# Layer 0's queries: x sent in by feature, with means and deviations sent through memory, in place of turning the normalised x on TensorE

## The chip, the cores and the metric

The kernel runs on one core of one Trainium2 chip. The time is device microseconds (us) of one execution, from its start to its end. Engines are named as the profile names them: PE (TensorE's matmuls), PEld (its weight loads), DVE (VectorE), ACT (ScalarE), POOL (GpSimd) and SP (SyncE, which issues most DMAs).

## The reference

Two layers of cross-attention and feed-forward over x of 2 x 2048 x 512, all float32. What matters here is layer 0's attention: its queries come from a doubly normalised x, its keys and values from a short context of 2 x 128 rows.

```python
def layer_norm(x, g, b):
    m = jnp.mean(x, axis=-1, keepdims=True)
    v = jnp.var(x, axis=-1, keepdims=True)
    return (x - m) * jax.lax.rsqrt(v + EPS) * g + b
...
q = layer_norm(query_sequences, ln_g, ln_b)      # query_sequences = _layernorm(x)
qh = (q @ Wq).reshape(N, t, N_HEADS, D_HEAD).transpose(0, 2, 1, 3)
qh = rope(qh); kh = rope(kh)
aw = jnp.einsum('nhtd,nhTd->nhtT', qh, kh) * (1.0 / jnp.sqrt(jnp.float32(D_HEAD)))
aw = GROK_SCALE * jnp.tanh(aw / GROK_SCALE)      # then the masks
out = jnp.einsum('nhtT,nhTd->nhtd', jax.nn.softmax(aw, axis=-1), vh)
return out @ Wo
...
x = x + _L0_xattn_ref(_layernorm(x, axis=-1), ctx_1024, ctx_1024, ...)
x = x + _L0_ffn_ref(_layernorm(x, axis=-1), ...)      # fake-quantised: needs the largest |x| of all tokens
x = x + _L1_xattn_ref(_layernorm(x, axis=-1), ctx_1024, ctx_1024, ...)
x = x + _L1_ffn_ref(_layernorm(x, axis=-1), ...)      # one of 8 experts for each token
```

## The kernel before

x stays in SBUF for the whole run as 32 tiles of 128 tokens x 512 features (`xs`), a token to a partition. A matmul sums over partitions, so the query product needs x the other way, a feature to a partition.

Layer 0's attention goes over 16 blocks of 256 tokens (two tiles; `blocks`, L312) and, in each block, over 4 groups of 4 heads. A block and a group make one *unit* u (block k = u // 4, group g = u % 4); there are 64. The loop at L479 is software-pipelined. In one pass it does scores(u), both query products of unit u + 2 (`queries`, L352: even features, then odd ones), mixed(u - 1), which weighs the values, and projected(u - 2), the output product, in that order on PE.

- `normed(k)` (L319) takes a block's mean and variance on DVE and the reciprocal deviation on POOL, `centered(k)` (L330) writes the normalised tile xn on DVE, and `turned(k, c0)` (L338) turns two of the four feature chunks: four 128x128 transposes on PE into PSUM (L345), from which ACT writes xnT with the layer norm's scale and bias (L347). For block k + 1, turned stands at the end of units g = 0 and g = 1 of block k; normed and centered stand in g = 2, one block earlier.
- The query product's two halves are multiplied by the rope tables on DVE (L367 to L373, tiles rt, one buffer each) and put together on POOL (L372, L374, tile q).
- In `mixed`, DVE takes the reciprocal (L410) and writes att (L411); scores and mixed share the PSUM tile sc.
- PSUM's pool psm has two buffers for one tag, "m", which the query products pq and the transposes pt share in turn.
- In g = 1 `finished` (L425) adds the attention to x and takes the next statistics, and `largest` (L433) takes each token's largest value for the FFN's quantisation.
- The FFN's weights are quantised beside this, one piece in the units g = 3 and g = 0 (`quantised`, L267; loads w_in with two buffers and w_down with one), and turned by DMA in the following unit (L290, L303).

Inside L456's block the order on PE, DVE and ACT is that of the program. The order on POOL and SP is the scheduler's: it takes what is ready by its own reckoning, so an instruction can go out long before its place in the program.

Before the loop, blocks 0 and 1 are prepared between the key and value products (L457 to L478); 23 of the x tiles hold weights until then and are loaded last (L474). After the loop, the FFN section loads the context again on ACT's queue (L611), turns it on PE (L623) and copies it to ctxT (L624) for layer 1's keys, two of which stand ahead of `act_step` (L648): that takes the maximum over all tokens, with one transpose (L590), which the FFN's first quantised tiles wait for.

Of the kernel before, what the change touches and what calls it, by code (L numbers as in the profile page):

```python
# [11 lines left out]
F32 = mybir.dt.float32  # L12
# [5 lines left out]
AF = mybir.ActivationFunctionType  # L18
ALU = mybir.AluOpType
# [4 lines left out]
P = 128  # L24
B, S, T, D = 2, 2048, 128, 512
# [37 lines left out]
def two_layers(ctx: ExitStack, tc: tile.TileContext, a, out):  # L63
# [9 lines left out]
    def load(dst, src):  # L73
        nc.sync.dma_start(out=dst, in_=src)
# [27 lines left out]
    def center(dst, x, mean, scale):  # L102
        nc.vector.tensor_scalar(dst, x, mean, scale, ALU.subtract, ALU.mult)
# [7 lines left out]
    def transposed(psum, src, n=ND):  # L111

        pt = psum.tile([P, n, P], F32, name="pt", tag="m")
        for c in range(n):
            nc.tensor.transpose(pt[:, c, :], src[:, c * P : (c + 1) * P], ident)
        return pt
# [33 lines left out]
    with ExitStack() as l0:  # L150
# [40 lines left out]
                wk[g].append(w.rearrange("p (c o f) -> p c o f", c=2, o=2))  # L191
        for n in order[:NB0]:
            load(xs[n], x_in[n])
        for c in range(ND):
            wv.append([])
            for f in range(E0 // D):
                w = xs[homes[8 + 2 * c + f]]
                load(w, a["L0_xattn_Wv"][c * P : (c + 1) * P, f * D : (f + 1) * D])
                wv[c].append(w)
# [79 lines left out]


        def gate_up_in(name, i):
            w = wtmp.tile([P, D], F32, name="w_in", tag="w_in")
            load(w, a[name][i * P : (i + 1) * P, :])
            return w

# [26 lines left out]
        blocks = [(j, b) for j in range(S // B0) for b in range(B)]  # L312
        tiles = [[b * TPB + j * NB0 + t for t in range(NB0)] for j, b in blocks]
        nu = len(blocks) * NG
        norms, xns, xnTs, ropes, qs, prs, atts, pws = {}, {}, {}, {}, {}, {}, {}, {}

        sc = pss.tile([P, 4, 512], F32, name="sc")

        def normed(k):  # L319


            for t, n in enumerate(tiles[k]):
                mv = variance(xs[n])
                ve = small.tile([P, 1], F32, name="ve")
                nc.vector.tensor_scalar(ve, mv[:, 1:2], 1.0 + EPS, EPS * EPS, ALU.mult, ALU.add)
                rr = small.tile([P, 1], F32, name="rr")
                nc.gpsimd.tensor_tensor(rr, ve, minus_half, ALU.pow)
                norms[k, t] = mv, rr

        def centered(k):  # L330
            xns[k] = []
            for t, n in enumerate(tiles[k]):
                mv, rr = norms[k, t]
                xn = mid.tile([P, D], F32, name="xn")
                center(xn, xs[n], mv[:, 0:1], rr)
                xns[k].append(xn)

        def turned(k, c0):  # L338

            if c0 == 0:  # L340
                xnTs[k] = mid.tile([P, ND, B0], F32, name="xnT")
            pt = psm.tile([P, 2, B0], F32, name="pt", tag="m")
            for c in range(2):
                for t, xn in enumerate(xns[k]):
                    nc.tensor.transpose(pt[:, c, t * P : (t + 1) * P], xn[:, (c0 + c) * P : (c0 + c + 1) * P], ident)  # L345
            for c in range(2):
                nc.scalar.activation(  # L347
                    xnTs[k][:, c0 + c, :], pt[:, c, :], AF.Identity,
                    bias=lnb[:, c0 + c : c0 + c + 1], scale=lng[:, c0 + c : c0 + c + 1],
                )  # L350

        def queries(u, par):  # L352
# [23 lines left out]
        def scores(u):  # L376

            k, g = divmod(u, NG)
            j, b = blocks[k]
            for par, k_ in ((0, kTe), (1, kTo)):  # L380
                for h in range(4):
                    rows = slice(32 * h, 32 * h + 32)
                    nc.tensor.matmul(  # L383
                        sc[:, h, :B0], k_[rows, g, b * T : (b + 1) * T], qs[u][par][rows, :],
                        start=(par == 0), stop=(par == 1), tile_position=(32 * h, 0),
                    )
            prs[u] = pr = mid.tile([P, 4, B0], F32, name="pr")
            nc.scalar.activation(pr, sc[:, :, :B0], AF.Tanh, scale=1.0 / (math.sqrt(DH0) * GROK))  # L388

            nc.scalar.activation(pr, pr, AF.Exp, bias=pad[:, b : b + 1], scale=GROK)  # L390
            if j == 0:
                nc.gpsimd.affine_select(
                    out=pr[:, :, :P], in_=pr[:, :, :P], pattern=[[0, 4], [1, P]],
                    compare_op=ALU.is_ge, fill=0.0, base=0, channel_multiplier=-1,
                )
# [60 lines left out]
        with tc.manual_schedule(engines={E.PE, E.DVE, E.Activation}):  # L456
            context()  # L457
            for g in range(NG):
                keys(g)
                if g == 1:  # L460
                    normed(0)
                if g == 2:
                    centered(0)
            nc.vector.tensor_scalar(pad, padu, -1e30, None, ALU.mult)
            for c in range(0, ND, 2):
                turned(0, c)
            values(0, 0)
            values(0, 1)
            queries(0, 0)
            values(1, 0)  # L470
            normed(1)
            queries(0, 1)
            values(1, 1)
            for n in homes:  # L474
                load(xs[n], x_in[n])
            queries(1, 0)
            centered(1)
            queries(1, 1)  # L478
            for u in range(nu + 2):  # L479
                k, g = divmod(u, NG)  # L480
                if u < nu:
                    scores(u)
                if u + 2 < nu:
                    queries(u + 2, 0)
                elif 1 < u < nu:
                    projected(u - 2, 0)
                if 0 < u <= nu:
                    mixed(u - 1)
                if u + 2 < nu:
                    queries(u + 2, 1)  # L490
                if u > 1:
                    for t in range(0 if u + 2 < nu or u >= nu else 1, NB0):
                        projected(u - 2, t)
                if g < 2 and k + 1 < nblk:
                    turned(k + 1, 2 * g)
                if u in turns:
                    turns[u]()
                if u in diags:
                    diags[u]()
                if g == 1 and k > 0:  # L500
                    for t in range(NB0):
                        finished(k - 1, t)
                    largest(k - 1, 0)
                if g == 2:
                    if k > 0:
                        largest(k - 1, 1)
                    if k + 2 < nblk:
                        normed(k + 2)
                        centered(k + 2)
                if g in (0, NG - 1) and u > 1:  # L510
                    if makes and not loaded:
                        load_, args, _, _ = makes[0]
                        loaded.append(load_(*args))
                    elif makes:
                        _, _, make, args = makes.pop(0)
                        turns[u + 1] = make(loaded.pop(), *args)
                        if makes:
                            load_, args, _, _ = makes[0]
                            loaded.append(load_(*args))
                if nu - 5 <= u < nu - 1:  # L520
                    diags[u + 1] = steps_along(u - nu + 5)
                if u == NG:
                    for name, clip in clips.items():
                        kept[name] = const.tile([P, 1], F32, name=f"kept_{name}")
                        nc.scalar.activation(kept[name], clip, AF.Exp, scale=-1.0)
                        nc.vector.tensor_scalar(kept[name], kept[name], 1.0, None, ALU.add)
                        nc.vector.reciprocal(kept[name], kept[name])
                if u == nu - 2:
                    load(wk1, a["L1_xattn_WkT"].rearrange("(c p) f -> p c f", p=P))
                    load(wv1, a["L1_xattn_WvT"].rearrange("(c p) f -> p c f", p=P))  # L530
            largest(nblk - 1, 1)
# [67 lines left out]
    with ExitStack() as up:  # L599
# [3 lines left out]
        kv = up.enter_context(tc.tile_pool(name="kv1", bufs=1, reuse_waits="tile"))  # L603

        ctxT = kv.tile([P, ND, B * T], F32, name="ctxT")
        cxs = [kv.tile([P, D], F32, name=f"cx{b}") for b in range(B)]
        bk = kv.tile([P, ND], F32, name="bk")
        bvb = kv.tile([P, D], F32, name="bvb")

        for b in range(B):  # L610
            nc.scalar.dma_start(out=cxs[b], in_=a["ctx_1024"][b])  # L611
        nc.scalar.dma_start(out=bk, in_=a["L1_xattn_bk"].rearrange("(c p) -> p c", p=P))
        load(bvb, a["L1_xattn_bv"].partition_broadcast(P))
        load(wq1, a["L1_xattn_WqT"].rearrange("(c p) f -> p c f", p=P))
# [4 lines left out]
        load(masks, a["mask_scores"].rearrange("(j p) k -> p j k", p=P))  # L619


        for b in range(B):
            pt = transposed(psm, cxs[b])  # L623
            nc.scalar.copy(ctxT[:, :, b * T : (b + 1) * T], pt)  # L624
        def keys(f):
            pk = psm.tile([P, B * T], F32, name="pk", tag="m")
            for c in range(ND):
# [656 lines left out]
```

## Time and profile before

| what | value |
|---|---|
| median of 3 runs | 1642.7 us (1641.58 to 1642.99) |
| profiled execution, its own time | 1642.48 us |
| its span | 1640.8 us |
| granted TensorE clock, mean | 0.998 |
| L345, the block transposes on PE | 128, a median of 273 ns each as recorded, from 27.5 to 623.1 us |
| L347, ACT's pass out of PSUM | 64, a mean of 559 ns, 32.6 us in all |
| L103, DVE's centering of xn | 32, 542 ns in the middle, 949 at most |
| layer 0's attention, last output matmul | starts 678.84 us, 7.13 us long (16 matmuls) |
| HBM read, written | 78.96 MB, 41.76 MB |

Matmuls are pipelined: a recorded duration is longer than the share of PE's time that the matmul takes, so the cost of a group of matmuls is read from the distance between what stands before and behind it. "Idle before" in the profile is the engine's idle time ahead of an instruction, with what ended it. DVE's and ACT's rows are durations of single instructions.

### The profile page before, as it was taken

What the parts mean: (1) busy time and instruction counts of PE and PEld (TensorE: products, weight loads), DVE (VectorE), ACT (ScalarE), POOL (GpSimd) and SP (SyncE); (2) the same over time, 40 slices, a digit from 0 to 9 for tenths busy, and PEclk for the clock granted to TensorE, in tenths of its full rate; (3) what the DMA queues carried; (4) which work ended last, traced back from release to release, by engine and by line L of the source; (5) the groups of instructions that cost most, each with busy time, mean ns of one, the idle gap of its engine ahead of it and who ended that gap; (6) DMA issues with size and microseconds to landing.
All of it is one profiled execution on the core that took longest, in us unless ns stands there. A gap on an engine that the chain in (4) does not pass through costs nothing. (4 is left out here: it accounts for less than half of the span.)

```text
span 1640.8 us, 26515 instructions
## 1 busy us (share of the span) xinstructions
PE 1597.7 (97%) x9962; PEld 952.5 (58%) x9962; DVE 1185.9 (72%) x2290; ACT 686.3 (42%) x1539; POOL 437.5 (27%) x498
## 2 busy tenths in 40 slices
PE   7999999999999999989999999999999999999997
PEld 5666666665666666534443566666666666654543
DVE  3466666777777765689986678898999889876332
ACT  1222222222222222234436576666666665662332
POOL 2322222222222221110005632333333221224553
PEclk9999999999999999999999999999999999999999
DMA  9400111010100220556658650001000000113332
GB/s 318 151 17 22 28 26 27 20 27 20 27 20 14 54 37 1 161 161 183 186 175 294 235 204 16 27 20 33 21 27 20 21 14 21 40 47 103 125 124 67
DMA packets 123883, 128.61 MB, mean 78 GB/s; under 512 B 43857, under 2 KB 91433, under 8 KB 123756
## 3 DMA queue, kind: packets, MB, share of 16 engines
q1 hardware_dynamic: 114508, 107.03, 21.2%
q0 software_dynamic: 6240, 18.70, 3.6%
q8 instruction: 80, 1.31, 0.3%
q10 hardware_dynamic: 3008, 1.19, 0.3%
q14 instruction: 47, 0.39, 0.1%
HBM read 78.96 MB, written 41.76 MB: 74 GB/s over the span
## 5 line engine op out<-in xcount | busy, mean ns | idle before, releaser
L362 PE MATMUL pq<-xnT,wq 128*128 128x256 f32 x1024 | 254.4, 392 | 0.0
L420 PE MATMUL pw<-wo,att 128*128 128x512 f32 x512 | 230.9, 593 | 0.0
L362 PEld LDWEIGHTS pq<-xnT,wq 128*128 128x128 f32 x1024 | 184.6, 190 | 66.9 <-issue 46.7
L855 ACT ACTIVATE s<-s,mx 128x128 f32<-128x128 f32 x512 | 176.7, 387 | 18.1 <-DVE mx L846 18.1
L388 ACT ACTIVATE pr<-sc 128x1024 f32<-128x1024 f32 x64 | 65.5, 1024 | 237.8 <-PE sc L383 234.7
L372 POOL TENSOR_TENSOR q<-rt,rt 128x256 f32<-128x256 f32 x64 | 46.5, 726 | 410.5 <-DVE rt L371 410.5
L420 PEld LDWEIGHTS pw<-wo,att 128*128 128x128 f32 x512 | 97.0, 190 | 96.2 <-issue 89.8
L410 DVE RECIPROCAL rd<-sc 128x256 f32<-128x256 f32 x64 | 112.5, 1757 | 51.1 <-PE sc L404 51.1
L1119 PE MATMUL pz<-we,x 128*128 x312 | 140.7, 594 | 0.6 <-issue 0.5
L813 PE MATMUL pq<-xT,wq 128*128 128x256 f32 x512 | 124.1, 385 | 0.0
L347 ACT ACTIVATE xnT<-pt,lnb,lng 128x256 f32<-128x256 f32 x64 | 32.6, 559 | 216.1 <-PE pt L345 216.1
L367 DVE TENSOR_TENSOR rt<-pq,rope_cos 128x256 f32<-128x256 f32 x64 | 27.2, 425 | 130.8 <-PE pq L362 120.2
L905 PE MATMUL pw<-wo,oT 128*128 128x512 f32 x256 | 115.5, 594 | 1.6 <-DVE oT L897 1.6
L928 PE MATMUL pl<-wgate,xnT 128*128 128x512 f32 x256 | 115.1, 592 | 0.0
L813 PEld LDWEIGHTS pq<-xT,wq 128*128 128x128 f32 x512 | 94.9, 190 | 28.0 <-issue 13.6
L716 ACT ACTIVATE gate<-pg,gsc 128x512 f32<-128x512 f32 x88 | 60.5, 687 | 96.5 <-PE pg L711 85.8
L711 PE MATMUL pu<-xqT,wuT 128*128 128x512 bf16 x352 | 90.3, 379 | 5.3 <-DVE h L719 5.3
L91 DVE BATCH_NORM_STATS2 st<-x 128x6 f32<-128x512 f32 x130 | 89.6, 689 | 5.6 <-DMA x<-in_ctx 3.4
L841 DVE SCALAR_TENSOR_TENSOR s<-sc,keep 128x1024 f32<-128x1024 f32 x64 | 77.9, 1217 | 20.6 <-PE sc L833 20.6
L1123 DVE TENSOR_TENSOR x<-x,x 128x512 f32<-128x512 f32 x39 | 27.0, 692 | 90.0 <-ACT x L1122 89.8
L711 PE MATMUL pg<-xqT,wgT 128*128 128x512 bf16 x352 | 90.3, 379 | 0.0
L1119 PEld LDWEIGHTS pz<-we,x 128*128 128x128 f32 x312 | 56.4, 190 | 58.2 <-issue 57.9
(218 smaller groups left out, 2847.7 us busy)
## 6 DMA issues: line engine op xcount, KB each, us to landing
h_dram<-h SPq DMA_DIRECT2D x88, 256.0 KB
hq<-h_dram SPq DMA_DIRECT2D x31, 704.0 KB
x_dram<-x SPq DMA_DIRECT2D x32, 258.0 KB
x<-in_x SPq DMA_DIRECT2D x32, 256.0 KB
we<-in_L_ffn_We SPq DMA_DIRECT2D x8, 1024.0 KB
w_in<-in_L_ffn_w_gate SPq DMA_DIRECT2D x11, 256.0 KB
w_down<-in_L_ffn_w_down SPq DMA_DIRECT2D x4, 704.0 KB
w_in<-in_L_ffn_w_up SPq DMA_DIRECT2D x11, 256.0 KB
```

What stands on the lines that cost most here:

```text
L91: nc.vector.bn_stats(out=st, in_=x)
L362: nc.tensor.matmul(pq, wqs[c // 2][:, c % 2, par, g * P : (g + 1) * P], xnTs[k][:, c, :], start=(c == 0), stop=(c == ND - 1))
L388: nc.scalar.activation(pr, sc[:, :, :B0], AF.Tanh, scale=1.0 / (math.sqrt(DH0) * GROK))
L410: nc.vector.reciprocal(rd, sc[:, 0, B0:])
L420: nc.tensor.matmul(pw, atts[u][:, f, t * P : (t + 1) * P], wo[:, 2 * g + f, :], start=(g == 0 and f == 0), stop=(g == NG - 1 and f == 1),)
L711: nc.tensor.matmul(dst, w[:, c, i * P : (i + 1) * P], xqTs[blk][:, c, :], start=(c == 0), stop=(c == ND - 1),)
L813: nc.tensor.matmul(pq, wq1[:, c, f * P : (f + 1) * P], xTs[blk][:, c, :], start=(c == 0), stop=(c == ND - 1))
L841: nc.vector.scalar_tensor_tensor(s, sc[:, 2 * half : 2 * half + 2].rearrange("p r c k -> p (r c) k"), -MASKED, keeps[n].unsqueeze(1).to_br ...
L855: nc.scalar.activation(s[:, h, :], s[:, h, :], AF.Exp, bias=mx[:, h : h + 1], **accum)
L905: nc.tensor.matmul(pw, os_[n][:, c, :], wo1[:, c, :], start=(c == 0), stop=(c == ND - 1))
L928: nc.tensor.matmul(pl, xn2T[n][:, c, :], wgate[:, c, :], start=(c == 0), stop=(c == ND - 1))
L1119: nc.tensor.matmul(pz, ring[j][:, c, :], we[:, bass.ds(e, 1), c, :], start=(c == 0), stop=(c == ND - 1))
```

## The change

x is sent in a second time by the host, already by feature (`x_turned`: for each block of 256 tokens, 128 features on partitions x 4 chunks x 256 tokens). For blocks 2 to 15 a block of it is loaded with one DMA of 512 KB straight into xnT (three buffers now). The mean and the reciprocal deviation are a value per token, which now lies along the free dimension: the block's 512 values are written to memory and read back spread over all partitions (tile along, one buffer). POOL subtracts the mean, DVE multiplies by the deviation, and ACT applies scale and bias in place. normed(k + 2), the load, the write and the read now stand at the end of g = 0 of block k; centered(k + 1) and scaled(k + 1) stand in g = 0 of block k, four units behind normed(k + 1), and affine(k + 1) in g = 1. Blocks 0 and 1 are still turned by PE (`first_blocks`), block 1's whole in unit 1. w_in has one buffer. In the FFN section the context too comes in by feature, as one DMA straight into ctxT, and its eight transposes and two copies go.

```diff
@@ -191,6 +191,13 @@
                 wk[g].append(w.rearrange("p (c o f) -> p c o f", c=2, o=2))
...
+        xnTs = {}
+
+        def features_in(k):
+
+            xnTs[k] = mid.tile([P, ND, B0], F32, name="xnT", bufs=3)
+            load(xnTs[k], a["x_turned"][k // B, k % B])
+
...
@@ -279,7 +286,7 @@
 
 
         def gate_up_in(name, i):
-            w = wtmp.tile([P, D], F32, name="w_in", tag="w_in")
+            w = wtmp.tile([P, D], F32, name="w_in", tag="w_in", bufs=1)
...
@@ -312,41 +319,64 @@
         blocks = [(j, b) for j in range(S // B0) for b in range(B)]
         tiles = [[b * TPB + j * NB0 + t for t in range(NB0)] for j, b in blocks]
         nu = len(blocks) * NG
-        norms, xns, xnTs, ropes, qs, prs, atts, pws = {}, {}, {}, {}, {}, {}, {}, {}
+        stats, along, ropes, qs, prs, atts, pws = {}, {}, {}, {}, {}, {}, {}
+        stat_dram = dram.tile([len(blocks), NB0, 2, P], F32, name="stat_dram")
 
...
         def normed(k):
 
 
+            stats[k] = small.tile([P, NB0, 2], F32, name="stat")
             for t, n in enumerate(tiles[k]):
                 mv = variance(xs[n])
                 ve = small.tile([P, 1], F32, name="ve")
                 nc.vector.tensor_scalar(ve, mv[:, 1:2], 1.0 + EPS, EPS * EPS, ALU.mult, ALU.add)
-                rr = small.tile([P, 1], F32, name="rr")
-                nc.gpsimd.tensor_tensor(rr, ve, minus_half, ALU.pow)
-                norms[k, t] = mv, rr
+                nc.vector.tensor_copy(stats[k][:, t, 0:1], mv[:, 0:1])
+                nc.gpsimd.tensor_tensor(stats[k][:, t, 1:2], ve, minus_half, ALU.pow)
+            if k > 1:
+                features_in(k)
+                turned_in(k)
+
+        def turned_in(k):
+
+            nc.sync.dma_start(out=stat_dram[k].rearrange("t s p -> p (t s)"), in_=stats[k].rearrange("p t s -> p (t s)"))
+            along[k] = mid.tile([P, NB0, 2, P], F32, name="along", bufs=1)
+            load(along[k], stat_dram[k].partition_broadcast(P))
+
+        def by_token(k, i, op, engine):
+            x = xnTs[k].rearrange("p c (t q) -> p c t q", t=NB0)
+            engine.tensor_tensor(x, x, along[k][:, :, i].unsqueeze(1).to_broadcast([P, ND, NB0, P]), op)
 
         def centered(k):
-            xns[k] = []
+            by_token(k, 0, ALU.subtract, nc.gpsimd)
+
+        def scaled(k):
+            by_token(k, 1, ALU.mult, nc.vector)
+
+        def first_blocks(k):
+
+            xn = mid.tile([P, NB0, D], F32, name="xn", tag="xnT", bufs=3)
             for t, n in enumerate(tiles[k]):
-                mv, rr = norms[k, t]
-                xn = mid.tile([P, D], F32, name="xn")
-                center(xn, xs[n], mv[:, 0:1], rr)
-                xns[k].append(xn)
-
-        def turned(k, c0):
-
-            if c0 == 0:
-                xnTs[k] = mid.tile([P, ND, B0], F32, name="xnT")
-            pt = psm.tile([P, 2, B0], F32, name="pt", tag="m")
-            for c in range(2):
-                for t, xn in enumerate(xns[k]):
-                    nc.tensor.transpose(pt[:, c, t * P : (t + 1) * P], xn[:, (c0 + c) * P : (c0 + c + 1) * P], ident)
-            for c in range(2):
+                center(xn[:, t, :], xs[n], stats[k][:, t, 0:1], stats[k][:, t, 1:2])
+            xnTs[k] = mid.tile([P, ND, B0], F32, name="xnT", bufs=3)
+
+            def rest():
+                for c0 in range(0, ND, 2):
+                    pt = psm.tile([P, 2, B0], F32, name="pt", tag="m")
+                    for c in range(2):
+                        for t in range(NB0):
+                            nc.tensor.transpose(
+                                pt[:, c, t * P : (t + 1) * P], xn[:, t, (c0 + c) * P : (c0 + c + 1) * P], ident
+                            )
+                    affine(k, c0, pt)
+
+            return rest
+
+        def affine(k, c0, pt=None):
+            for c in range(c0, c0 + 2):
                 nc.scalar.activation(
-                    xnTs[k][:, c0 + c, :], pt[:, c, :], AF.Identity,
-                    bias=lnb[:, c0 + c : c0 + c + 1], scale=lng[:, c0 + c : c0 + c + 1],
+                    xnTs[k][:, c, :], xnTs[k][:, c, :] if pt is None else pt[:, c - c0, :], AF.Identity, bias=lnb[:, c : c + 1], scale=lng[:, c : c + 1]
                 )
 
...
@@ -460,10 +490,9 @@
                 if g == 1:
                     normed(0)
                 if g == 2:
-                    centered(0)
+                    turn = first_blocks(0)
...
-            for c in range(0, ND, 2):
-                turned(0, c)
+            turn()
...
@@ -474,12 +503,13 @@
             for n in homes:
                 load(xs[n], x_in[n])
             queries(1, 0)
-            centered(1)
             queries(1, 1)
             for u in range(nu + 2):
                 k, g = divmod(u, NG)
                 if u < nu:
                     scores(u)
+                if g == 0 and 0 < k < nblk - 1:
+                    centered(k + 1)
                 if u + 2 < nu:
                     queries(u + 2, 0)
                 elif 1 < u < nu:
@@ -491,8 +521,13 @@
                 if u > 1:
                     for t in range(0 if u + 2 < nu or u >= nu else 1, NB0):
                         projected(u - 2, t)
-                if g < 2 and k + 1 < nblk:
-                    turned(k + 1, 2 * g)
+                if u == 0:
+                    turn = first_blocks(1)
+                if u == 1:
+                    turn()
+                elif g == 1 and k + 1 < nblk:
+                    for c in range(0, ND, 2):
+                        affine(k + 1, c)
                 if u in turns:
                     turns[u]()
                 if u in diags:
@@ -504,9 +539,6 @@
                 if g == 2:
                     if k > 0:
                         largest(k - 1, 1)
-                    if k + 2 < nblk:
-                        normed(k + 2)
-                        centered(k + 2)
                 if g in (0, NG - 1) and u > 1:
...
@@ -519,6 +551,11 @@
                             loaded.append(load_(*args))
                 if nu - 5 <= u < nu - 1:
                     diags[u + 1] = steps_along(u - nu + 5)
+                if g == 0:
+                    if 0 < k < nblk - 1:
+                        scaled(k + 1)
+                    if k + 2 < nblk:
+                        normed(k + 2)
...
@@ -603,12 +640,10 @@
         kv = up.enter_context(tc.tile_pool(name="kv1", bufs=1, reuse_waits="tile"))
 
         ctxT = kv.tile([P, ND, B * T], F32, name="ctxT")
-        cxs = [kv.tile([P, D], F32, name=f"cx{b}") for b in range(B)]
...
-        for b in range(B):
-            nc.scalar.dma_start(out=cxs[b], in_=a["ctx_1024"][b])
+        nc.scalar.dma_start(out=ctxT, in_=a["ctx_turned"])
...
@@ -619,9 +654,6 @@
         load(masks, a["mask_scores"].rearrange("(j p) k -> p j k", p=P))
 
 
-        for b in range(B):
-            pt = transposed(psm, cxs[b])
-            nc.scalar.copy(ctxT[:, :, b * T : (b + 1) * T], pt)
...
@@ -1252,6 +1284,9 @@
 
     arrays = {k: np.asarray(v) for k, v in inputs.items()}
     arrays["mask_pad"] = arrays.pop("mask_BxS2_bf0")
+
+    arrays["x_turned"] = arrays["x"].reshape(B, S // B0, B0, ND, P).transpose(1, 0, 4, 3, 2)
+    arrays["ctx_turned"] = arrays["ctx_1024"].reshape(B * T, ND, P).transpose(2, 1, 0)
     arrays["mask_scores"] = arrays.pop("mask_1x1xSxS2_bk0").reshape(S, T)
 
     for name in ("L0_xattn_Wq", "L0_xattn_Wk"):
```

## The prediction

> **What bounds the kernel now.** I read the page's busy shares first, then the busy time in four windows of one block of layer 0, then TensorE's timeline at the end of that stage.
>
> ```profile
> PE 1597.7 (97%) x9962; PEld 952.5 (58%) x9962; DVE 1185.9 (72%) x2290; ACT 686.3 (42%) x1539; POOL 437.5 (27%) x498
> PE   7999999999999999989999999999999999999997
> ```
>
> TensorE is busy in every slice but the first and the last, so time goes only where its own list shortens or where it must wait. The four units (head groups) of one block:
>
> ```profile
> 292.80:303.03 10.23, 10.23 (x70) 6.30 (x69) 5.81 (x12) 3.19 (x4) 1.50 (x3) 1.00 0.16 39
> 303.03:312.82 9.79, 9.79 (x66) 5.80 (x65) 8.50 (x16) 3.19 (x4) 2.83 (x4) 1.00 0.01 2
> 312.82:322.61 9.79, 9.79 (x66) 5.80 (x65) 8.11 (x19) 2.17 (x2) 2.75 (x4) 1.00 0.00 0
> 322.61:332.83 10.22, 10.22 (x69) 6.30 (x68) 5.69 (x11) 2.17 (x2) 1.41 (x2) 1.00 0.18 40
> ```
>
> After the length come the busy times of PE, PEld, DVE, ACT and POOL. PE is busy all of every window, the granted clock is 1.00, and DVE, next, is busy 28.1 of 40.0 us. Two units last 9.79 us and two about 10.22; the long ones end with the transposes:
>
> ```profile
> 602.84 0.71 PE L383 MATMUL sc<-q,kTe 32*128 32x256 f32 x8
> ...
> 612.54 0.60 PE L345 MATMUL pt<-ident,xn 128*128 128x128 f32 x4
> 613.07 0.71 PE L383 MATMUL sc<-q,kTe 32*128 32x256 f32 x8
> ...
> 622.76 0.60 PE L345 MATMUL pt<-ident,xn 128*128 128x128 f32 x4
> 623.29 0.71 PE L383 MATMUL sc<-q,kTe 32*128 32x256 f32 x8
> ...
> 633.08 0.71 PE L383 MATMUL sc<-q,kTe 32*128 32x256 f32 x8
> ```
>
> From one unit's scores to the next: 10.23 and 10.22 with a group of four transposes, 9.79 without (623.29 to 633.08). A group costs 10.225 - 9.79 = 0.435 us, though its matmuls read 0.60.
>
> **What is removed.** Blocks 2 to 15 lose their transposes: 14 blocks x 2 groups x 0.435 = **12.2 us**, all on the engine that sets the end.
>
> **The start.** Block 1's two groups now both stand in unit 1, and DVE does the two centerings (1.00 us at 49.52) and normed(2) (2.09 us, as at 312.27, plus two copies at 0.07) after unit 0's last rope product at 55.98. The sum 3.23 takes it to 59.2, so unit 1's first rope product, at 58.74 now, is 0.5 late; both end at 60.05, just before the reciprocal (60.20 now). PE gets through unit 1's second query group at 61.4 (0.44 earlier, since a group left unit 0). The first four transposes take the buffer freed at 60.05; the other four need that of the second query product, which DVE reads behind reciprocal and att, until about 63.2. The next scores start at 63.85 instead of 62.83: **+1.0 us**. Bounds: 0 if DVE is not late, 3.2 if all its moved work is paid.
>
> **Into layer 0's FFN.** The eight context transposes start at 685.81 and hold the keys until their copies:
>
> ```profile
> 685.81 1.04 PE L115 MATMUL pt<-ident,cx 128*128 128x128 f32 x8
> 687.65 3.72 PE L628 MATMUL pk<-ctxT,wq 128*128 128x256 f32 x16 [0.80 <-ACT ctxT L624]
> 691.21 0.27 PE L590 MATMUL pm<-ident,mb 128*128 128x128 f32 x1
> 691.94 3.72 PE L628 MATMUL pk<-ctxT,wq 128*128 128x256 f32 x16 [0.46 <-ACT kT L631]
> ```
>
> The first keys could start 1.84 us earlier, but the transpose at 691.21 waits for DVE's chain of the maximum (the last projected matmul, add, statistics, largest, mb at 690.97), which doesn't move. What is left is the 0.46 behind it: **-0.5 us**. This wants the 512 KB context in place by 685.8. The present loads go out at 676.82 and 679.00 and their packets are through by about 682; by the tile sizes the new tile lies over the last-but-one probabilities and a query tile, both free by 674.6. Bounds: -1.84, and +2.5 if the load must wait for the last projection at 685.97 (issue to last packet about 3 to 4 us, as those loads took).
>
> **What is added, and its cover.** *ScalarE* does as many affine passes, from SBUF instead of PSUM, at 0.56 us as now (0.47 in the nearest row, the keys' bias). Four in unit g=1 after the exponential (done 3.4 us into the unit) end at 5.7; the queries want them 5 us later. Nothing.
>
> *POOL's centering*, 1024 elements a partition, isn't in the trace. The 256-element subtraction takes 0.73 and the 512-element add 1.27 us alone, so 2.35; where DVE works beside it that add takes 1.85 in the middle, which gives 3.4. POOL is idle 8.4 us of a unit ("8.38 <-DVE rt L371"). Queued behind it are q's two halves, then DVE's next rope products, which overwrite what q reads: q ends 9.0 us into a unit, the products start at 13.3. Nothing, if its operands are there.
>
> *DVE*: scaled costs 1.22 (128x1024 row, L841; twice that if POOL is in its way), the copies 0.14; two centerings (1.1) go. In g=0 after its last rope product it now has quantise 2.06 + scaled 1.22 + normed 2.23 = 5.5 us, where a 9.79 unit leaves 5.2 until the next rope product; g=1 carries its 5.25 as now; g=2, from which normed left, recovers. So DVE is 0.3 us late for a unit. PE would notice only when att is late: it is done 7.1 us into a unit, the next scores want it at 9.79, and 0.7 idle stands ahead of the reciprocal. Slack 3.4. The two g=0 units with a w_down quantise (3.77) are about 2.0 late, still inside. Nothing; cover gone, each us over 3.4 is a us on PE.
>
> *The rule against it.* Beside DVE, the 512-element add on POOL grew from 1.27 to 1.85, and DVE's 0.54 centering to 0.95 at most. The Trainium skill (GPSIMD Engine Reference, section Specifications) says that the two engines share SBUF interfaces, with contention when DVE has two SBUF inputs. That is what scaled has. By the rule it and q slow each other; by the rows the extra is at most 1.2 us, inside 3.4.
>
> *SP and the DMAs.* A block adds a 512 KB load, a write of 512 four-byte pieces and a 256 KB broadcast; the load's slot is free three units before. Nearest rows: the v_dram write is issued at 705.38 and the broadcast that reads it at 707.01, and POOL uses that at 711.22: 5.9 us in all against a lead of 4 units (39 us). In the window 684 to 688 two 2 KB loads in such pieces make 1071 packets within about 1.5 us. The Trainium skill (DMA: Bandwidth & Descriptors, section Rules for kernel authors) says that such a last dimension gives one descriptor per element; by it the write could be the slow link, by the rows it is not. Behind the write SP holds quantised weights' transposes, first used at 698.7. With one w_in buffer the next weight loads only after a quantise: 322.6, wanted 330.3, a load taking about 2.5. Nothing.
>
> **Sum.** -12.2 + 1.0 - 0.5 = -11.7 us on the profiled execution's 1642.48 (span 1640.8 and 1.7 around it) is 1630.8. The median shown is 0.2 above it: **1631.0**. Later stages stay PE-bound and move whole.
>
> **Rivals.**
> *Slower: POOL stands in front of q.* SP and POOL need not keep program order: the w_down load is issued at 54.31, its call stands in unit 47. If centered comes on POOL where its broadcast is expected and that is late, q waits, then DVE's rope, then att, then scores. Free are 4.3 - 2.35 = 2.0 on POOL and 3.4 on DVE; each us beyond costs 14 us in the run. Against: one round trip is 5.9. The gain of 0.83 a block is gone at a wait of 6.2 us; at 8 (5.9 plus 2 behind a 704 KB load) the run is (8 - 5.4) x 14 - 11.7 = 25 longer, 1667. Chance 0.08.
> *Partly eaten*: DVE or POOL late by 0.1 to 0.5 us of PE time a block, since g=0 and g=1 have no room together: 14 x 0.3 = 4, 1635 (1632.5 to 1638). For it: 5.5 and 5.25 against 5.2. Chance 0.13.
> *Context late*: the 0.5 turns into +2.5: 1634. Chance 0.07.
> *No gain*: the unit is held by something the transposes hid, and stays at 10.2; 1642. Against: units without transposes stand at 9.79 throughout. Chance 0.04.
> *Forecast*: 0.68, 1628.4 (no loss at the start, 1.84 at the end) to 1633.
>
> **Numbers.** 0.2% is 3.3 us, about what a measurement of this kernel can tell from no change. Faster 0.68 + 0.13 + 0.07 = 0.88, same 0.04, slower 0.08. The range runs from 1628.4 to 1637, over most of the partly eaten case.
>
> **What would show it.** All of blocks 1 to 15's units at 9.79 us between scores, none at 10.2: right; a unit at 10 or more with PE waiting on att or q: the second rival, and at 12 or more the first. Between unit 1's transposes a gap of about 1.3 us. The first keys within 0.5 us of the last projection, then a wait of about 1.8 before the maximum's transpose. POOL's centering 2.3 to 3.4 us, idle before it put down to no DMA. PE waits on along or xnT would make it wrong.

## The result, and the profile after

The changed kernel takes 1762.9 us (median of 4 runs, 1761.7 to 1765.3) against 1642.8 before: the ratio is 1.0737, 95% interval 1.0721 to 1.0753. Forecast were 1631.0 and a range up to 1637.0. The profiled execution took 1765.3 us (span 1763.6).

The lines of the page that answer to the first two shown of before, and the granted clock in the same 40 slices:

```profile
PE 1617.1 (92%) x9842; PEld 956.7 (54%) x9842; DVE 1188.1 (67%) x2308; ACT 684.2 (39%) x1537; POOL 465.3 (26%) x512
PE   7888988888888889899999999999999999999997
PEclk9999989999989999899999999999999999999999
```

TensorE's matmuls are 120 fewer, but it is no longer busy throughout: 14 of the first 17 slices, which lie in layer 0's attention, read 8 where they read 9 before, and the clock dips in three of them. No other engine fills up in their place. TensorE's timeline shows where, by the first scores of successive units (bracket: idle time before the instruction, and what ended it):

```profile
102.38 0.71 PE L413 MATMUL sc<-q,kTe 32*128 32x256 f32 x8
...
112.17 0.71 PE L413 MATMUL sc<-q,kTe 32*128 32x256 f32 x8
...
128.91 1.24 PE L413 MATMUL sc<-q,kTe 32*128 32x256 f32 x8 [6.87 <-DVE att L441]
...
140.35 0.71 PE L413 MATMUL sc<-q,kTe 32*128 32x256 f32 x8
```

Units without a wait last 9.79 us (102.38 to 112.17), as forecast; none lasts 10.2. But once in each of the 14 changed blocks the next scores wait 6 to 9 us for att, and the unit behind that wait takes 11.4 (128.91 to 140.35; 11.3 to 12.8 in all) instead of 9.79. Why att is late is read backwards from the same stretch on DVE and POOL:

```profile
105.65 0.56 POOL L336 TENSOR_TENSOR stat<-ve,minus_half 128x1 f32<-128x1 f32 x1 [0.52 <-DVE stat L335]
...
120.19 2.34 POOL L349 TENSOR_TENSOR xnT<-xnT,along 128x1024 f32<-128x1024 f32 x1 [13.39 <-DMA along<-stat_dram]
122.49 0.72 POOL L402 TENSOR_TENSOR q<-rt,rt 128x256 f32<-128x256 f32 x1
...
123.86 1.17 POOL L100 TENSOR_TENSOR rstd<-ve,minus_half 128x1 f32<-128x1 f32 x2
124.44 0.55 DVE L103 TENSOR_SCALAR xn<-x,mean,rstd 128x512 f32<-128x512 f32 x1 [10.20 <-POOL rstd L100]
...
128.07 0.69 DVE L441 TENSOR_TENSOR att<-sc,rd 128x512 f32<-128x512 f32 x1
```

POOL finished block 3's statistics at 106.2, and the next thing it does but for one mask is block 3's *centering*, which the program has four units later. It stands idle 13.4 us for the broadcast along. Behind it on POOL are q and the reciprocal deviations rstd of `finished`; DVE waits 10.2 us for rstd with the next rope products, reciprocal and att behind that; PE waits for att. What the broadcast itself waited for stands on SP:

```profile
106.23 0.40 SPq L343 DMA_DIRECT2D stat_dram<-stat  x1
114.61 0.33 SPq L74 DMA_DIRECT2D along<-stat_dram  x1
115.03 0.37 SPq L74 DMA_DIRECT2D xnT<-in_x_turned  x1
```

The write of 512 four-byte values is issued at 106.23; the read that needs it goes out 8.4 us later, and POOL has its data 5.6 us after that: 14.0 us, for which the forecast had 5.9. The packets of the write had ended by about 107.6, so 7 of the 8.4 us pass with no packet of any DMA moving.

Over the 14 blocks the waits are (waiter, releaser: us in all, times, longest):

```profile
DVE xn L103 <- POOL rstd L100: 137.9, 13, 12.0
...
POOL xnT L349 <- DMA along<-stat_dram: 111.1, 8, 15.1
PE sc L413 <- DVE att L441: 103.3, 14, 9.2
...
POOL xnT L349 <- issue: 80.4, 6, 15.0
```

POOL's two rows are one wait, 191.5 us or 13.7 a block (for six of them the releaser wasn't found). By the unit starts PE loses 104.3 us waiting in front of scores, and the 14 units just behind those waits are together 29.7 us longer than 14 of 9.79. The second sum is the clock; here are busy times in stretches around the wait above, the granted clock third from the end:

```profile
122.00:128.90 6.90, 0.03 (x1) 0.03 (x1) 4.39 (x7) 0.00 (x0) 3.52 (x6) 0.76 0.00 0
128.90:129.90 1.00, 0.99 (x9) 0.91 (x13) 1.00 (x3) 0.00 (x0) 0.66 (x1) 0.50 0.00 0
...
132.00:133.00 1.00, 1.00 (x5) 0.86 (x4) 0.00 (x0) 0.97 (x2) 0.00 (x0) 0.81 0.00 0
133.00:134.00 1.00, 1.00 (x11) 0.48 (x14) 0.27 (x1) 0.31 (x1) 0.57 (x1) 1.00 0.06 16
```

The 0.76 of the idle stretch is 1.00 in its first 3.4 us and 0.52 in the rest. After 6.9 us of idle PE runs at half its clock for about 3.5 us, and the eight scores take 1.24 instead of 0.71. In half of the blocks the half clock lasts longer: behind the wait that ends at 225.18 it is 0.50 for 3.4 us and 0.59 for the next 3.4.

### The profile page after: what moved, and what is told of

The parts are those of the page before. It is cut to its first block, busy times and chain, and to the rows that moved or that the text cites. A ratio compares the mean times of both kernels' runs of the same rounds, so it can differ in the third digit from the quotient of the medians.

```text
span 1763.6 us, 26440 instructions
## 1 busy us (share of the span) xinstructions
PE 1617.1 (92%) x9842; PEld 956.7 (54%) x9842; DVE 1188.1 (67%) x2308; ACT 684.2 (39%) x1537; POOL 465.3 (26%) x512
## 5 line engine op out<-in xcount | busy, mean ns | idle before, releaser
L392 PE MATMUL pq<-xnT,wq 128*128 128x256 f32 x1024 | 270.5, 410 | 0.0
L392 PEld LDWEIGHTS pq<-xnT,wq 128*128 128x128 f32 x1024 | 195.4, 201 | 75.4 <-issue 48.9
L413 PE MATMUL sc<-q,kTe 32*128 32x256 f32 x512 | 53.0, 487 | 104.0 <-DVE att L441 104.0
L103 DVE TENSOR_SCALAR xn<-x,mean,rstd 128x512 f32<-128x512 f32 x32 | 22.4, 702 | 137.9 <-POOL rstd L100 137.9
L413 PEld LDWEIGHTS sc<-q,kTe 32*128 32x128 f32 x512 | 23.3, 210 | 149.7 <-issue 125.2
```

Of the source, the lines that this page charges most:

```text
L392: nc.tensor.matmul(pq, wqs[c // 2][:, c % 2, par, g * P : (g + 1) * P], xnTs[k][:, c, :], start=(c == 0), stop=(c == ND - 1))
L413: nc.tensor.matmul(sc[:, h, :B0], k_[rows, g, b * T : (b + 1) * T], qs[u][par][rows, :], start=(par == 0), stop=(par == 1), tile_position= ...
```

## The experiments

The theory: POOL's order has the centering right behind the statistics, so that POOL stands for the 14 us round trip in front of q and rstd. The first rival is that DVE is over-full in g = 0 and g = 1, the second that SP or the single w_in buffer makes something late. Both were terms of the forecast, costed at nothing. Each run's time stands beside the kernel before on the same chip.

| run | time, us | before, us | ratio (95%) |
|---|---|---|---|
| e1 POOL in program order | 1630.7 (4 runs) | 1641.4 | 0.9929 (0.9914 to 0.9945) |
| e2 pieces of 16 bytes | 1641.0 (8) | 1641.4 | 0.9996 (0.9986 to 1.0006) |
| e3 centering on DVE | 1631.7 (4) | 1641.4 | 0.9933 (0.9918 to 0.9948) |
| e4 context alone | 1641.7 (11) | 1641.4 | 1.0000 (0.9991 to 1.0009) |
| e5 lead of one unit | 1761.5 (2) | 1641.6 | 1.0730 (1.0710 to 1.0749) |
| e6 lead of two units | 1629.3 (2) | 1641.6 | 0.9924 (0.9906 to 0.9942) |
| e7 small writes | 1628.4 (1) | 1641.6 | a single run |
| e8 start as before | 1630.7 (5) | 1641.6 | 0.9931 (0.9918 to 0.9945) |

**e1, POOL held to program order.**

```diff
-        with tc.manual_schedule(engines={E.PE, E.DVE, E.Activation}):
+        with tc.manual_schedule(engines={E.PE, E.DVE, E.Activation, E.Pool}):
```

> The changed kernel with POOL too held to program order, so that centered(k+1) stands in unit 4k, four units behind normed(k+1), and no longer right behind the statistics that it waits for. All instructions are the same. Theory (POOL stands in front of q and rstd until the broadcast is there): no wait on along, all units 9.79 us, 1630 to 1634 us. Rival (DVE is over-full in g = 0 and g = 1, or SP with one w_in buffer is late): the stalls stay, 1740 us or more.

It takes 1630.7 us, with the same instructions as the changed kernel. Its units from the third to the 60th last 9.79 us without exception, and the centering finds its data there; it comes straight behind q, with no wait in front. POOL, DVE and SP in e1:

```profile
159.40 0.72 POOL L404 TENSOR_TENSOR q<-rt,rt 128x256 f32<-128x256 f32 x1
160.08 2.53 POOL L349 TENSOR_TENSOR xnT<-xnT,along 128x1024 f32<-128x1024 f32 x1
```

```profile
160.44 2.45 DVE L284 TENSOR_SCALAR wb<-w_in 128x512 bf16<-128x512 f32 x1
```

```profile
135.36 0.38 SPq L343 DMA_DIRECT2D stat_dram<-stat  x1
143.48 0.33 SPq L74 DMA_DIRECT2D along<-stat_dram  x1
```

The write still takes 8.1 us to be read, and now costs nothing. Nor does the centering's effect on DVE: the cast of the FFN weights (wb), which takes 0.43 us elsewhere, takes 2.45 beside it in each of 11 blocks. DVE's work, SP's chain and the single w_in buffer are as in the changed kernel, so both rivals fall. The profiled executions differ by 1765.3 - 1630.8 = 134.5 us; the waits and the slow clock above make 104.3 + 29.7 = 134.0.

**e2, the statistics in pieces of 16 bytes**, POOL's order free as in the changed kernel.

```diff
-        stat_dram = dram.tile([len(blocks), NB0, 2, P], F32, name="stat_dram")
+        stat_dram = dram.tile([len(blocks), P, NB0, 2], F32, name="stat_dram")
...
-            along[k] = mid.tile([P, NB0, 2, P], F32, name="along", bufs=1)
+            along[k] = mid.tile([P, P, NB0, 2], F32, name="along", bufs=1)
```

> The changed kernel, POOL's order as it is, but the statistics are written as one piece of 16 bytes a partition (128 pieces in place of 512 of 4 bytes) and read back with a stride. If the 8.4 us from the write's issue to the read's issue come from the number or the size of the pieces, this falls to 2 to 4 us, POOL's wait from 13.4 to 7 to 9, the stall of a block from about 8.6 to 2 to 4, and the time to 1660 to 1700 us. If they are a fixed price of a write to memory that a read follows, nothing changes: 1755 us or more.

1641.0 us: better than expected, and the same as before within 0.15%. The write is read after 1.4 us in nine of the 14 blocks (2.9 at most), on SP:

```profile
138.20 0.33 SPq L343 DMA_DIRECT2D stat_dram<-stat  x1
139.61 0.33 SPq L74 DMA_DIRECT2D along<-stat_dram  x1
```

POOL then waits only 5.7 us a block (6.7 at most), and PE's waits in front of scores fall from 104.3 to 11.2 us. The stride costs the centering 2.93 instead of 2.34 and DVE's multiplication 2.02 instead of 1.22. This is small beside what the run shows: with POOL in the wrong place, 7 us less of round trip are worth 120 us.

**e3, the centering on DVE**, which keeps program order.

```diff
         def centered(k):
-            by_token(k, 0, ALU.subtract, nc.gpsimd)
+            by_token(k, 0, ALU.subtract, nc.vector)
```

> The changed kernel with the subtraction on DVE, which keeps program order, in place of POOL. Theory (POOL's place in the order is the cause): nothing on POOL waits for along, no stall; DVE has 1.2 us more in g = 0 (6.7 us against a room of 5.2), inside its slack of 3.4: 1630 to 1636 us. Rival (DVE over-full): slower than the changed kernel, above 1765 us.

1631.7 us. All units from the third to the 60th last 9.79 us with 1.2 us more on DVE, in the unit that had the least room. So DVE's slack is real, and it was never DVE's amount of work.

**e4, the context alone** sent in by feature, on the kernel before.

```diff
-        for b in range(B):
-            nc.scalar.dma_start(out=cxs[b], in_=a["ctx_1024"][b])
+        nc.scalar.dma_start(out=ctxT, in_=a["ctx_turned"])
...
-        for b in range(B):
-            pt = transposed(psm, cxs[b])
-            nc.scalar.copy(ctxT[:, :, b * T : (b + 1) * T], pt)
```

> The kernel before with only the context sent in by feature. The key products start up to 1.84 us earlier, but the maximum's transpose still waits for DVE: 0.5 to 0.8 us less, 1641.9 to 1642.3 us.

No difference that 11 runs tell (interval 0.9991 to 1.0009, about 1.5 us either way). Its trace has the expected shape:

```profile
677.70 7.13 PE L420 MATMUL pw<-wo,att 128*128 128x512 f32 x16
684.67 3.62 PE L623 MATMUL pk<-ctxT,wq 128*128 128x256 f32 x16
689.97 0.30 PE L590 MATMUL pm<-ident,mb 128*128 128x128 f32 x1 [1.68 <-DVE bq L679]
```

The keys follow the last projection at once, and the maximum's transpose then waits 1.7 us on DVE. From the last projection's start to the FFN's first matmul it is 19.1 us, 19.9 before: 0.8 less, too little for the timing.

**e5 and e6, the lead.** POOL held to program order as in e1, the centering written one or two units behind the statistics in place of four.

```diff
-                if g == 0 and 0 < k < nblk - 1:
-                    centered(k + 1)
+                if g == 1 and k + 2 < nblk:      # e6: g == 2
+                    centered(k + 2)
```

> POOL held to program order as in the run with POOL's order fixed, but centered(k+2) written one unit behind normed(k+2), ahead of that unit's q: the place that the changed kernel had it in. Theory: about 13 us of wait on POOL in each of 14 blocks, stalls as in the changed kernel, 1755 to 1770 us. Rival (something else in the freely ordered kernel made it slow, such as SP's order): near 1631 us.

> The same with centered(k+2) two units behind normed(k+2). The statistics leave about 13 us into unit g = 0, the broadcast is there some 14 us later, at 27 to 28; POOL is free from 22 and q of unit g = 2 wants it at 27.0, so q comes some 3 us late, inside POOL's and DVE's slack of 5.4 us: 1630 to 1634 us. If the slack is worth less than worked out: a stall in each block, 1640 us or more.

With one unit's lead it takes 1761.5 us, the changed kernel's time within 0.1%, with waits for att in the same 14 units; with two, 1629.3. Nothing else in the program moved. At the place shown of the changed kernel POOL waits 13 us in e5 and PE 6.5:

```profile
128.55 1.24 PE L413 MATMUL sc<-q,kTe 32*128 32x256 f32 x8 [6.53 <-DVE att L441]
```

In e6 POOL still waits 4.3 us here (5.5 in the mean), ahead of q, and PE doesn't notice: all units from the third to the 60th last 9.79 (POOL, then DVE):

```profile
148.80 2.35 POOL L349 TENSOR_TENSOR xnT<-xnT,along 128x1024 f32<-128x1024 f32 x1 [4.29 <-DMA along<-stat_dram]
151.09 0.92 POOL L402 TENSOR_TENSOR q<-rt,rt 128x256 f32<-128x256 f32 x1
```

```profile
149.28 2.14 DVE L103 TENSOR_SCALAR xn<-x,mean,rstd 128x512 f32<-128x512 f32 x1
```

In e6 no rstd stands behind the waiting centering (POOL did that block's two at 141.93 and 143.72), and q starts 1.9 to 3.4 us later than in e1 in 11 blocks and up to 5.7 in the other three. The forecast had worked out a slack of 5.4.

**e7, small writes by themselves**, in e1, in a unit where SP issues little else.

```diff
+                pieces = {2: (4, 1, 1), 3: (4, 1, 16), 4: (4, 1, 128), 5: (2, 2, 2), 6: (1, 4, 4), 7: (1, 1, 1), 8: (4, 1, 1), 9: (1, 4, 128)}
...
+                n, width, step = pieces[k]
+                at = dram.tile([n, P, step], F32, name=f"probe{k}")
+                nc.sync.dma_start(out=at[:, :, :width].rearrange("n p w -> p n w"), in_=...)
+                load(back, at[0, 0:1, 0:1])
```

> A measurement by itself, in the kernel with POOL's order fixed: in unit g = 2 of blocks 2 to 9 one extra small write to memory and a read that waits for it, both unused. Pieces of 4 bytes: 512 side by side, 512 at 64 bytes' distance, 512 at 512 bytes' distance; 256 of 8; 128 of 16; 128 of 4; 512 of 4 again; 128 of 16 at 512 bytes' distance. Read: issue of the write to issue of the read. If it is the number of pieces: about 8 us for 512, 4 for 256, 2 for 128 whatever their size and distance. If neighbours in one line get in each other's way: the spread pieces are faster, about 2 to 3 us. If size alone: all 4-byte cases alike. The run's time should be that of the kernel without it, 1630 to 1632 us.

SP's queue, the first, the third and the sixth write, each with the read that waits for it (the table's last column is what all DMAs moved between the two):

```profile
150.45 0.37 SPq L354 DMA_DIRECT2D probe<-src  x1
161.05 0.30 SPq L74 DMA_DIRECT2D back<-probe  x1
...
228.77 0.37 SPq L354 DMA_DIRECT2D probe<-src  x1
230.55 0.24 SPq L74 DMA_DIRECT2D back<-probe  x1
...
346.25 0.33 SPq L354 DMA_DIRECT2D probe<-src  x1
354.52 0.25 SPq L74 DMA_DIRECT2D back<-probe  x1
```

| pieces | distance in memory | write to read, us | moved meanwhile, MB |
|---|---|---|---|
| 512 of 4 bytes | side by side | 10.6, again 10.3 | 0.02, 0.07 |
| 512 of 4 bytes | 64 bytes | 2.9 | 0.64 |
| 512 of 4 bytes | 512 bytes | 1.8 | 0.03 |
| 256 of 8 bytes | side by side | 4.3 | 0.74 |
| 128 of 16 bytes | side by side | 1.4 | 0.02 |
| 128 of 4 bytes | side by side | 8.3 | 0.41 |
| 128 of 16 bytes | 512 bytes | 3.3 | 0.36 |

Neither number nor size alone makes the price: 512 pieces of 4 bytes are the fastest but one when they are far apart, and 128 side by side nearly as slow as 512. What is slow is small pieces that are neighbours. That they get in each other's way while one line of memory is rewritten would fit, but no run looks inside the memory. Four of the eight readings were taken while the rope tables' loads still moved (0.36 to 0.74 MB, last column), so they are no more than upper bounds, the 3.3 of the last row among them; the readings without that traffic are 10.6, 10.3, 1.8 and 1.4. The 8.3 stays a slow one: its traffic ended 2.1 us after the write's issue.

**e8, block 1 prepared as before**, in e1.

```diff
             queries(1, 0)
+            turn = first_blocks(1)
             queries(1, 1)
...
-                if u == 0:
-                    turn = first_blocks(1)
-                if u == 1:
-                    turn()
+                if u < 2:
+                    turn([2 * u])
```

> POOL's order fixed, and block 1's centering and its two transpose groups back where the kernel before had them (ahead of the loop; units 0 and 1). This undoes the loss at the start: from unit 0's to unit 3's scores 22.2 us in place of 23.1, 0.8 to 0.9 us less in all, 1629.5 to 1630.5 us, which a timing hardly tells but the unit starts do.

From unit 0's scores to unit 3's it is 22.22 us against 23.08 in e1, as expected; the time, 1630.7, can't tell it. In e1 the gap that the forecast had between unit 1's transposes is there, 1.1 us, but it is ended by another engine:

```profile
62.41 0.66 PE L369 MATMUL pt<-ident,xn 128*128 128x128 f32 x4 [1.11 <-ACT xnT L378]
```

The second group starts at 62.41, while DVE's last read of the query product runs only from 62.43. It waits for ACT's two passes over the first group's own buffer.

## Why the prediction was wrong, point by point

- *-12.2 us for the transposes*: right. All units are at 9.79 in e1; nothing had hidden behind them.
- *+1.0 at the start*: 0.9 by e1 and e8. The size was right, the wait another (ACT's pass, not DVE's read).
- *-0.5 into the FFN*: 0.8 in the traces of e1 and e4, not resolvable in the times.
- *DVE, ScalarE, SP behind the write, one w_in buffer: nothing*: right, by e1 and e3. POOL's centering takes 2.34 us, where 2.35 was worked out, and 2.53 in e1 beside DVE; DVE's 1.22 is exact in 13 of 14 blocks, 1.70 beside POOL's q in the other.
- *"the extra is at most 1.2 us"*, beside POOL: too small, and looked for in scaled and q. In e1 it was the cast wb, with one input, that POOL's centering held up, by 2.0 us a block (2.45 against 0.43). That too stayed inside the 3.4, so no time came of it.
- **The step that failed: "5.9 us in all against a lead of 4 units (39 us)".** Both halves were wrong. The lead was read from the program, and only PE, DVE and ACT keep to the program there; on POOL the centering stood directly behind the statistics, which is no lead. And the round trip was taken from a write of 512-byte rows (1.6 us from write to read), where 512 neighbouring pieces of 4 bytes take 8.4, and the read 5.6 behind it instead of 4.2. The 4-byte loads of the window 684 to 688, put beside it as the nearest thing, were reads of memory and not writes, and their packets' time says nothing on when a write is done. Of the two halves the lead decides: with it the long round trip costs nothing (e1), without it even a short one uses up the gain (e2).
- *The slower rival* named this mechanism and its place, and its arithmetic held: a free wait of 5.4 us, break-even at 6.2. e2, at 5.7 us a block with a centering 0.6 slower, is where gain and loss cancel. At the measured 13.7 us it gives (13.7 - 5.4) x 14 = 116 us, where PE's waits were 104.3. It lacked two things: rstd, which stands behind the centering on POOL too and stopped DVE before q did; and the clock, 29.7 us. Its chance was 0.08 because the round trip was believed to be 5.9.
- The forecast's own evidence against the lead, a load issued some 460 us ahead of its place in the program (54.31, where unit 47 starts at 512.98), was written down under the rival and not carried into the main sum.

The sum itself, 1630.8 for the profiled execution, is e1's 1630.8: the forecast describes the kernel whose POOL keeps the order in which it was written. That the two agree to a tenth is luck: e1's four runs lie between 1629.1 and 1631.0, and two small terms, +1.0 and -0.5, were 0.9 and -0.8.

## What to carry to other kernels

A lead is worth what the engine's real order gives it: for every engine whose order a scheduler chooses, ask where the waiting instruction can come at the earliest, and price the whole wait there with all that is queued behind it. A round trip through memory is priced by a write of the same shape, down to how its pieces lie, and should not stand in front of something that feeds the bounding engine. If it must be there, two units of lead were enough here, and so was another engine.

## What the runs showed of the hardware

- Small writes to memory are slow when they are neighbours: 512 pieces of 4 bytes side by side were ready for reading after 8.1 to 10.9 us in all runs that write them, 512 bytes apart after 1.8 in e7. The Trainium skill (DMA: Bandwidth & Descriptors, section Specifications) puts a limit at 512 bytes, below which the engine reads, changes and writes back. By that alone 4-byte pieces should cost the same near or far; e7's 10.3 against 1.8 us says that distance counts, and the measurement decides.
- A wait of PE's costs more than its length: the granted clock was 1.00 in the first 3.4 us of an idle stretch of 6.9 and 0.52 in the rest; behind waits of 6 to 9 us it stayed at half for 3 to 6 us, 1.5 to 3 us lost each time; after 2.45 us of idle in e2 the next unit lasted 9.79. The Trainium skill (TensorE: Matmul & The Clock Gate, section Part 1: The HAM clock gate) gives a window of about 3.4 us, idle for which the clock is halved until a busy one has passed; the rows agree from both sides.
- DVE's centering, 0.54 us alone, took 2.14 us in e6 when it began inside POOL's 2.35 us subtraction, and ended 0.3 us after it. In e1 the cast wb, 0.43 us alone, began inside the same subtraction in 11 blocks, took 2.45 each time and ended 0.3 us after it. Both were held for as long as POOL's instruction ran. In e6 DVE's reductions (0.69) and rope products (0.41) kept their length beside it.
